# Layer 0's expert tiles in an order written out by hand, and one logarithm per image in the preparation for the scans

## The chip, the core and the metric

The kernel runs on one core of one Trainium2 chip, as one program. Its engines are called PE (matrix multiplication; its weight loads are shown apart, as PEld), DVE (vector), ACT (scalar functions), POOL (GpSimd) and SP (which issues DMAs). The metric is the device time of one execution in microseconds (us); lower is better.

## The reference

Four images of 256 channels and 32 × 32 pixels pass through two layers; each is a token mixer followed by a mixture of experts, and all is float32.

- Layer 0 mixes by attention with a kept set of scores, a depthwise convolution and a projection. Layer 1 mixes by four selective scans over the pixels (along rows and columns, forward and back), whose results are averaged.
- A mixture of experts normalizes each token, chooses two of eight experts for it, and adds their weighted results to the token: 256 to 256 to 256 features in layer 0, 256 to 1024 to 256 in layer 1.

The part that the change touches, in short:

```
# layer 0's experts
h = gelu(tokens @ w1[e] + b1[e])
y = h @ w2[e] + b2[e]
out = out + combine[:, e] * y

# the selective scan of layer 1
delta = softplus(x @ W_delta + b_delta)     # log(1 + exp(.))
Bm, Cm = x @ W_B, x @ W_C
dA  = exp(delta * -exp(A_log))
dBx = (delta * x) * Bm
h   = scan(dA, dBx)                         # h[l] = dA[l] * h[l-1] + dBx[l]
y   = sum_n(h * Cm) + x * D
```

## The kernel before

**Layout.** Channels lie on the 128 partitions in two halves (CT = 2), the 1024 pixels of an image along them, often in two halves of 512 (NHALF). An image is 8 blocks of 128 tokens (NT).

**Stages.** The attention of all images runs until about 1900 us of the span, layer 0's normalization, routing and scatter until about 2045, the 36 expert tiles of layer 0 until about 2276, the scans until about 3560, layer 1's experts and the end after that.

**Who sets the order.** A tile framework takes the program as written and, outside marked stretches, lets a planner order the instructions of all engines by priorities and a model of their costs. Inside `tc.manual_schedule()` each engine keeps the order of the source. Before the change, only the scans (L1792) are such a stretch. Each engine runs its own queue in order; semaphores join the queues. Tiles of a pool with `bufs=n` rotate through n buffers, and a new use waits for the last reader of the old one. Pools opened after others were closed take over their memory.

**Routing and scatter (L1244, L1123, L1498).** For each image, the tokens are normalized, their experts chosen, and POOL copies each token by indirect DMA to two slots in DRAM (`slots_x0`), grouped by expert.

**The tiles of layer 0 (`tile0`, L1507 to L1550).** A tile is 256 slots of one expert. SP reads the block's number and the expert's into registers and loads the tokens `xs` (L1514) and the two weights `w` (L1517, L1519). DVE copies the expert's biases (L1521, L1523) and works out the weight of each token (L1525 to L1528). PE transposes the tokens (`tp`, L1532), DVE copies them (`xe`, L1534); PE multiplies by w1 (`hp`, L1539), ACT takes the gelu (`hid`, L1540); PE multiplies by w2 (`yp`), DVE adds the bias (`ys`, L1546), ACT multiplies by the token's weight (L1548), DVE combines with the token where its best expert is this one (L1549), and SP stores the block to `slots_y0` (L1550). `xs` and `ys` have 4 buffers, the weights 3.

**The streams beside the tiles (L1565 to L1581).** Python generators whose steps are written between the tiles, four per tile. From tile 15 on there is `whole(0)`: the 16 gathers of image 0 from `slots_y0` on POOL (`fetched`, L1444, two per step; the first eight write, the others add), eight empty steps, and the transposes of the result with their addition to the image (`completed`, L1459; `op` at L1464). It is followed by the preparation of image 0 for its scans (`Prep.steps`, L1332). From tile 23 on there is `whole(1)`. Images 2 and 3 are gathered during the first scans.

**The preparation (`Prep.steps`, L1332 to L1442, 40 steps).** It normalizes the image over its channels: means on PE (L1341), squares on ACT, variances on PE, a power on POOL (L1359) refined on DVE, the scale spread by PE (`rb`), then the products with W_B and W_C (`bp`). The rest is softplus, worked out as relu(z) + log(1 + exp(-|z|)) with a correction for what rounding 1 + v loses: with v = exp(-|z|), `lost` forms v + 1 and the part of v that the sum dropped. For each channel half: PE forms z (`zp`), ACT takes Relu, Abs and Exp, DVE `lost` (L1419 to L1421), ACT one Ln over 128 × 1024 (L1430), DVE and POOL add up delta (L1434, L1435). Last, POOL forms dx = delta * x (L1393) and DVE adds x * D (L1394).

**The scans (L1739 to L1796).** Each of the 128 turns runs the scans of one image, channel half and state: column, forward and backward scans on DVE (L1697, L1671, L1680), exponentials on ACT, the products `uu` (L1658) and `da_c` (L1691) on POOL, sums on PE. The preparation of the next image runs beside them, two steps per turn, from an image's first turn for image 1 and from its ninth for images 2 and 3.

Of the kernel before, what the change touches and what calls it, by code (L numbers as in the profile page):

```python
# [11 lines left out]
F32 = mybir.dt.float32  # L12
# [9 lines left out]
P = 128  # L22
# [39 lines left out]
def metaformer(ctx: ExitStack, tc: tile.TileContext, t: dict, out: bass.AP):  # L62
# [1259 lines left out]
    class Prep:  # L1322
# [9 lines left out]
        def steps(self, room, psum, tag):  # L1332
# [44 lines left out]
            bc = room("sp", [4 * HALF])[: 2 * NS, :L]  # L1377
# [12 lines left out]
            def rest(c):  # L1390
                for h in range(NHALF):
                    cols = ts(h, HALF)
                    nc.gpsimd.tensor_tensor(self.dx[:, c, cols], self.delta[:, c, cols], xm[:, c, cols], ALU.mult)  # L1393
                    nc.vector.scalar_tensor_tensor(x[b][:, c, cols], xm[:, c, cols], dsk[:, c : c + 1],  # L1394
                                                   x[b][:, c, cols], ALU.mult, ALU.add)
                    yield
                    yield

            behind = iter(())
            for c in range(CT):  # L1400
                sp = room("sp", [4 * HALF]).rearrange("p (k n) -> p k n", k=4)

                def begin(h):
                    cols = ts(h, HALF)
                    zp = psum.tile([P, HALF], F32, tag=tag, name="zp")
                    for k in range(CT):
                        nc.tensor.matmul(zp, wd[:, k, ts(c, P)], xm[:, k, cols],
                                         start=(k == 0), stop=(k == CT - 1))
                    next(behind, None)
                    yield  # L1410
                    nc.scalar.activation(self.delta[:, c, cols], zp, AF.Relu, bias=bd[:, c : c + 1])
                    nc.scalar.activation(sp[:, h], zp, AF.Abs, bias=bd[:, c : c + 1])
                    nc.scalar.activation(sp[:, h], sp[:, h], AF.Exp, scale=-1.0)
                    next(behind, None)
                    yield

                def lost(h):
                    v, up, dd = sp[:, h], sp[:, 2 + h], self.dx[:, c, ts(h, HALF)]
                    nc.vector.tensor_scalar(up, v, 1.0, None, ALU.add)  # L1419
                    nc.vector.scalar_tensor_tensor(dd, up, 1.0, v, ALU.subtract, ALU.subtract, reverse1=True)  # L1420
                    nc.vector.scalar_tensor_tensor(v, v, 2.0, dd, ALU.subtract, ALU.mult)  # L1421

                yield from begin(0)
                yield from begin(1)
                for _ in behind:
                    pass
                lost(0)
                lost(1)
                yield
                nc.scalar.activation(sp[:, 2:], sp[:, 2:], AF.Ln)  # L1430
                yield
                for h in range(NHALF):
                    dd = self.delta[:, c, ts(h, HALF)]
                    nc.vector.scalar_tensor_tensor(dd, sp[:, h], -0.5, dd, ALU.mult, ALU.add)  # L1434
                    nc.gpsimd.tensor_tensor(dd, dd, sp[:, 2 + h], ALU.add)  # L1435
                yield
                yield
                behind = rest(c)
            for _ in behind:
                yield  # L1440
            yield
            yield  # L1442
# [31 lines left out]
    with ExitStack() as st:  # L1474
        wp = st.enter_context(tc.tile_pool(name="m0_w", bufs=1))
        pb = st.enter_context(tc.tile_pool(name="m0_b", bufs=2))
# [3 lines left out]

        b1 = load(wp, "b1_0", [P, E, CT])
        b2 = wp.tile([P, E, C], F32, tag="b2_0", name="b2_0")
        nc.sync.dma_start(b2, t["b2_0"].rearrange("e d -> (e d)").partition_broadcast(P).rearrange(
            "p (e d) -> p e d", e=E))
        tokens = [wp.tile([P, NT, W0], F32, tag=f"tok{b}", name=f"tok{b}") for b in range(B)]
        scattered = nc.alloc_semaphore("scattered")
        for b in range(B):
            d = pb.tile([P, CT, L], F32, tag="d", name="d")
            here = slot0[:, :, ts(b, NT)]
            for _ in norm(b, 0, tokens[b], pb, ps_n, "t", "t", d):  # L1490
                pass
            for _ in route(b, 0, tokens[b], here, wp.tile([P, 2560], F32, tag="numbers", name="numbers"), ps_n, "t"):
                pass

            with tc.tile_critical(name=f"scatter{b}", no_gpsimd_drain=True):
                for n in range(NT):
                    for k in range(2):
                        nc.gpsimd.indirect_dma_start(  # L1498
                            out=slots_x0, out_offset=bass.IndirectOffsetOnAxis(ap=here[:, k, n : n + 1], axis=0),
                            in_=tokens[b][:, n], in_offset=None).then_inc(scattered, 16)  # L1500
                nc.gpsimd.wait_ge(scattered, 16 * 2 * NT * (b + 1))
                if b == B - 1:
                    nc.clear_and_free_semaphores([scattered])

        blocks_x, blocks_y = (a.rearrange("(k a p) c -> k p a c", a=T // P, p=P) for a in (slots_x0, slots_y0))

        def tile0(i):  # L1507
            def register(k, most, engines):
                return nc.values_load(every.which[0:1, k, i : i + 1], engines=engines, min_val=0, max_val=most,
                                      skip_runtime_bounds_check_because="the minimum with that of a count")  # L1510

            block = register(1, E * BLOCKS, [mybir.EngineType.SP])
            xs = pb.tile([P, T // P, W0], F32, tag="xs", name="xs", bufs=4)
            nc.sync.dma_start(xs, blocks_x[bass.ds(block, 1)].rearrange("o p a c -> p (o a) c"))  # L1514
            e = register(0, E - 1, [mybir.EngineType.SP, mybir.EngineType.DVE])
            w1 = pb.tile([P, CT, C], F32, tag="w1", name="w1", bufs=3)
            nc.sync.dma_start(w1, t["w1_0"][bass.ds(e, 1)].rearrange("o (c p) f -> p (o c) f", p=P))  # L1517
            w2 = pb.tile([P, CT, C], F32, tag="w2", name="w2", bufs=3)
            nc.sync.dma_start(w2, t["w2_0"][bass.ds(e, 1)].rearrange("o (c p) f -> p (o c) f", p=P))  # L1519
            b1e = pb.tile([P, CT], F32, tag="b1e", name="b1e")  # L1520
            nc.vector.tensor_copy(b1e, b1[:, bass.ds(e, 1)].rearrange("p o c -> p (o c)"))  # L1521
            b2e = pb.tile([P, C], F32, tag="b2e", name="b2e")
            nc.vector.tensor_copy(b2e, b2[:, bass.ds(e, 1)].rearrange("p o d -> p (o d)"))  # L1523
            best = pb.tile([P, T // P], F32, tag="best", name="best")
            nc.vector.tensor_scalar(best, xs[:, :, C], every.expert[:, i : i + 1], None, ALU.is_equal)  # L1525
            wt = pb.tile([P, T // P], F32, tag="wt", name="wt")
            nc.vector.tensor_tensor(wt, best, xs[:, :, C + 1], ALU.mult)
            nc.vector.tensor_tensor(wt, wt, xs[:, :, C + 2], ALU.add)  # L1528
            tp = ps1.tile([P, CT, T], F32, tag="tp", name="tp")
            for a in range(T // P):  # L1530
                for c in range(CT):
                    nc.tensor.transpose(tp[:, c, ts(a, P)], xs[:, a, ts(c, P)], ident)  # L1532
            xe = pb.tile([P, CT, T], F32, tag="xe", name="xe")
            nc.vector.tensor_copy(xe, tp)  # L1534
            hp = ps_h.tile([P, CT, T], F32, tag="hp", name="hp")
            hid = pb.tile([P, CT, T], F32, tag="hid", name="hid")
            for f in range(CT):
                for c in range(CT):
                    nc.tensor.matmul(hp[:, f], w1[:, c, ts(f, P)], xe[:, c], start=(c == 0), stop=(c == CT - 1))  # L1539
                nc.scalar.activation(hid[:, f], hp[:, f], AF.Gelu, bias=b1e[:, f : f + 1])  # L1540
            yp = ps1.tile([P, T // P, C], F32, tag="yp", name="yp")
            for a in range(T // P):
                for f in range(CT):
                    nc.tensor.matmul(yp[:, a], hid[:, f, ts(a, P)], w2[:, f, :], start=(f == 0), stop=(f == CT - 1))
            ys = pb.tile([P, T // P, C], F32, tag="ys", name="ys", bufs=4)
            nc.vector.tensor_tensor(ys, yp, b2e.unsqueeze(1).to_broadcast([P, T // P, C]), ALU.add)  # L1546
            for a in range(T // P):
                nc.scalar.mul(ys[:, a], ys[:, a], wt[:, a : a + 1])  # L1548
                nc.vector.scalar_tensor_tensor(ys[:, a], xs[:, a, :C], best[:, a : a + 1], ys[:, a], ALU.mult, ALU.add)  # L1549
# [463 lines left out]
```

## Time and profile before

| | |
|---|---|
| Median of 3 runs | 4160.04 us (4149.68 to 4175.9) |
| Profiled execution | 4157.79 us, span 4155.8 us, 50303 instructions |
| PE busy | 3518.4 us (85%) |
| DVE busy | 3041.4 us (73%) |
| ACT busy | 2847.3 us (69%) |
| POOL busy | 1823.3 us (44%) |
| Tiles of layer 0 | about 2045 to 2276 us of the span |
| Scans | about 2276 to 3560 us of the span |

How to read it: times in the views are us, and the share of busy time is of the whole span, so it averages stages with different limits. "idle before <-releaser" is the time in which an engine stood still ahead of an instruction, and what ended it. SPq, POOLq and the like are the queues of an engine that issue DMAs. A stretch is a part of the span between two times in us; its columns are the length, the busy time of each engine with the number of instructions, the clock granted to PE as a share of full speed, the busy share of the DMA engines, and GB/s. Lines of the time line give start, length, engine, source line, operation and operands, the number of equal neighbours, and in brackets the idle time before them. Lines of the waits give the waiting instruction, what it waited for, the total, the number of times and the longest.

### The profile page before, as it was taken

The page shows a single profiled execution, that of the slowest core. Times are in us where ns is not written, and L with a number is a line of the kernel's source. Part 1 is how long each engine was busy: PE and PEld are TensorE (multiplying, and loading weights), DVE is VectorE, ACT ScalarE, POOL GpSimd, SP SyncE. Part 2 cuts the span into 40 slices and gives each one's busy share as a digit, 9 for nine tenths or more (in the row PEclk, how much of TensorE's full clock was granted, in tenths as well). Part 3 has the DMA queues.
Part 4 walks back from the last instruction along what each step waited for, and adds up shares of the span by engine and source line. Part 5 has one row for each costly group of instructions (what it writes and reads, how often), then busy time and mean ns, then how long its engine had stood idle before and what let it go on. Part 6 is the DMA issues. An engine that isn't in the chain of part 4 may idle for free. (4 is left out here: it accounts for less than half of the span.)

```text
span 4155.8 us, 50303 instructions
## 1 busy us (share of the span) xinstructions
PE 3518.4 (85%) x17502; PEld 1949.6 (47%) x17502; DVE 3041.4 (73%) x5327; ACT 2847.3 (69%) x3823; POOL 1823.3 (44%) x1436
## 2 busy tenths in 40 slices
PE   8378878888888888866487999999999999999996
PEld 5144434444444444433365434443443434688885
DVE  2689899989898989883356889899899899411112
ACT  2889999999999999963235667767667677422222
POOL 0146454554455445562323666446446546221111
PEclk9568888788778877977698999999999999999997
DMA  9300093009000000001375334333333334565565
GB/s 289 92 1 1 1 263 79 1 1 306 32 1 1 11 1 1 11 1 45 118 200 167 120 104 132 102 107 114 109 100 114 118 103 136 185 186 184 188 196 184
DMA packets 280986, 426.37 MB, mean 103 GB/s; under 512 B 31889, under 2 KB 223634, under 8 KB 280594
## 3 DMA queue, kind: packets, MB, share of 16 engines
q1 hardware_dynamic: 259920, 382.66, 30.3%
q0 software_dynamic: 17024, 38.98, 3.0%
q8 instruction: 141, 2.31, 0.2%
q10 hardware_dynamic: 3778, 1.41, 0.1%
q14 instruction: 123, 1.01, 0.1%
HBM read 280.34 MB, written 142.64 MB: 102 GB/s over the span
## 5 line engine op out<-in xcount | busy, mean ns | idle before, releaser
L490 POOL TENSOR_SCALAR dr<-s_n,last 128x1024 bf16<-128x1024 f32 x256 | 732.1, 2878 | 853.9 <-DVE state L518 435.4
L406 ACT ACTIVATE junk_a<-s_n,state 128x1024 int8<-128x1024 f32 x448 | 514.6, 1149 | 25.4 <-DVE state L518 6.8
L1691 POOL TENSOR_TENSOR da_c<-prod,come 128x1024 f32<-128x1024 f32 x128 | 248.1, 1938 | 386.7 <-DVE h L1697 381.9
L410 DVE TENSOR_SCALAR_CACHE_REDUCE junk_v<-s_n,state 128x1024 int8<-128x1024 f32 x320 | 408.7, 1277 | 8.8
L1861 ACT ACTIVATE hid<-hp,b 128x256 f32<-128x256 f32 x288 | 133.7, 474 | 355.1 <-PE hp L1859 354.6
L457 DVE SCALAR_TENSOR_TENSOR w<-s_n,win 128x1024 f32<-128x1024 f32 x256 | 351.4, 1373 | 5.3
L460 DVE MAX8 win<-w 128x8 f32<-128x1024 f32 x256 | 314.5, 1228 | 8.8
L1658 POOL TENSOR_TENSOR uu<-dx,bb 128x1024 f32<-128x1024 f32 x128 | 304.9, 2382 | 1.0 <-DMA bb<-bc_d 1.0
L558 ACT ACTIVATE ex<-sT 128x1024 f32<-128x1024 f32 x256 | 247.0, 1015 | 84.5 <-PE sT L550 84.4
L1697 DVE TENSOR_TENSOR_SCAN h<-da_c,uu 128x1024 f32<-128x1024 f32 x128 | 302.8, 2366 | 0.0
L406 ACT ACTIVATE junk_a<-s_n,guess 128x1024 int8<-128x1024 f32 x256 | 294.2, 1149 | 7.4
L1671 DVE TENSOR_TENSOR_SCAN h<-da,uu 128x1024 f32<-128x1024 f32 x128 | 290.8, 2272 | 4.2 <-POOL uu L1658 4.2
L1680 DVE TENSOR_TENSOR_SCAN h<-da,uu 128x1024 f32<-128x1024 f32 x128 | 289.8, 2264 | 0.0
L568 PE MATMUL o_ps<-ex,vT 128*32 128x256 f32 x2048 | 238.1, 445 | 45.4 <-ACT ex L558 37.4
L1701 PE MATMUL hp<-h,ident 128*128 128x512 f32 x512 | 248.9, 609 | 31.1 <-DVE h L1697 30.6
L1645 ACT ACTIVATE da_c<-delta,a_log 128x1024 f32<-128x1024 f32 x128 | 268.2, 2096 | 0.2
L1859 PE MATMUL hp<-xe,w 128*128 128x256 f32 x1152 | 258.6, 381 | 6.1 <-DVE xe L1847 5.9
L1666 PE MATMUL hp<-da_c,ident 128*128 128x512 f32 x512 | 247.0, 605 | 18.2 <-POOL da_c L1691 16.3
L440 ACT COPY s_n<-sp 128x1024 f32<-128x1024 f32 x256 | 245.6, 1004 | 24.4 <-PE sp L432 12.5
L1870 DVE TENSOR_TENSOR ys<-yp,b2e 128x512 f32<-128x512 f32 x36 | 24.9, 691 | 321.1 <-PE yp L1867 321.1
L1666 PE MATMUL hp<-h,twice 128*128 128x512 f32 x512 | 243.8, 599 | 17.3 <-issue 13.4
L1659 ACT COPY uu<-uu 128x1024 f32<-128x1024 f32 x128 | 254.5, 1988 | 3.4 <-POOL uu L1658 3.4
(542 smaller groups left out, 7519.8 us busy)
## 6 DMA issues: line engine op xcount, KB each, us to landing
bb<-bc_d SPq DMA_DIRECT2D x128, 512.0 KB
cb<-bc_d SPq DMA_DIRECT2D x128, 512.0 KB
w<-in_w SPq DMA_DIRECT2D x36, 1024.0 KB
w2e<-in_w SPq DMA_DIRECT2D x36, 1024.0 KB
slots_x<-zeros SPq DMA_DIRECT2D x1, 33411.0 KB
slots_x<-zeros SPq DMA_DIRECT2D x1, 33282.0 KB
slots_y<-zeros SPq DMA_DIRECT2D x1, 33024.0 KB
w<-in_w SPq DMA_DIRECT2D x72, 256.0 KB
```

Source lines behind the costliest of these rows:

```text
L406: nc.scalar.activation(junk, self.row(r), AF.Sign, bias=thr, scale=-1.0, accum_out=u)
L410: nc.vector.tensor_scalar(junk, self.row(r), thr, None, ALU.is_lt, ALU.add, accum_out=u)
L457: nc.vector.scalar_tensor_tensor(w, self.row(r), self.win[:, r, 0:1], self.row(r), ALU.is_gt if r < LAST_DVE else ALU.is_ge, ALU.subtract, ...
L460: nc.vector.max(out=self.win[:, r, 1:], in_=w)
L490: ins = nc.gpsimd.tensor_scalar(dr, self.row(r), self.last[:, r : r + 1], None, ALU.is_lt)
L1645: nc.scalar.activation(grid(self.da_c), cols_flipped(self.prep.delta[:, self.c]), AF.Exp, scale=self.decay)
L1658: nc.gpsimd.tensor_tensor(self.uu[:, 0], self.prep.dx[:, self.c], self.bb, ALU.mult)
L1666: nc.tensor.matmul(self.hp[h], ident if eye is None else eye, view[:, ts(h, HW // NHALF), :], start=first, stop=last)
L1671: nc.vector.tensor_tensor_scan(rows.rearrange("p r w -> p (r w)"), self.da, self.uu[:, 0], 0.0, ALU.mult, ALU.add)
L1680: nc.vector.tensor_tensor_scan(hs[:, ::-1], self.da[:, ::-1], self.uu[:, 0][:, ::-1], 0.0, ALU.mult, ALU.add)
L1697: nc.vector.tensor_tensor_scan(hs, self.da_c, self.uu[:, 1], 0.0, ALU.mult, ALU.add)
L1859: nc.tensor.matmul(hp[:, f % 2], self.w1[:, c, ts(f, P)], self.xe[:, c], start=(c == 0), stop=(c == CT - 1))
```

## The change

It has two parts.

1. **The tiles.** `tile0` becomes a class `Tile0` with six steps (`load`, `turned`, `small`, `hidden`, `result`, `store`), and the 36 tiles and their streams stand in `tc.manual_schedule()`. Iteration i writes hidden(i), store(i-1), turned(i+1), result(i), small(i+1), load(i+3), and then three steps of each stream that has begun. `store` issues its DMA from POOL, which loads the block's number itself; DVE loads the expert's number with an instruction of its own. `xs` has 6 buffers, the weights 4, `ys` 8. `whole` gathers four per step. The normalization, routing and scatter use pools of their own, closed before those of the tiles are opened, with a smaller `numbers`.
2. **The preparation.** The four parts (channel half, pixel half) run in one sequence: `lost` takes two DVE instructions and leaves the lost part in dx; one Ln covers 128 × 2048 and adds the one itself (`bias=1.0`); the additions, the product dx and the addition to x are on DVE alone. It has 44 steps.

```diff
-            behind = iter(())
-            for c in range(CT):
-                sp = room("sp", [4 * HALF]).rearrange("p (k n) -> p k n", k=4)
...
-                def lost(h):
-                    v, up, dd = sp[:, h], sp[:, 2 + h], self.dx[:, c, ts(h, HALF)]
-                    nc.vector.tensor_scalar(up, v, 1.0, None, ALU.add)
-                    nc.vector.scalar_tensor_tensor(dd, up, 1.0, v, ALU.subtract, ALU.subtract, reverse1=True)
-                    nc.vector.scalar_tensor_tensor(v, v, 2.0, dd, ALU.subtract, ALU.mult)
...
-                nc.scalar.activation(sp[:, 2:], sp[:, 2:], AF.Ln)
-                yield
-                for h in range(NHALF):
-                    dd = self.delta[:, c, ts(h, HALF)]
-                    nc.vector.scalar_tensor_tensor(dd, sp[:, h], -0.5, dd, ALU.mult, ALU.add)
-                    nc.gpsimd.tensor_tensor(dd, dd, sp[:, 2 + h], ALU.add)
+            parts = [(c, ts(h, HALF)) for c in range(CT) for h in range(NHALF)]
+            v = room("sp", [CT, L])
+
+            def lost(c, cols):
+                back = self.dx[:, c, cols]
+                nc.vector.tensor_scalar(back, v[:, c, cols], 1.0, 1.0, ALU.add, ALU.subtract)
+                nc.vector.tensor_tensor(back, v[:, c, cols], back, ALU.subtract)
+
+            for i, (c, cols) in enumerate(parts):
+                zp = psum.tile([P, HALF], F32, tag=tag, name="zp")
+                for k in range(CT):
+                    nc.tensor.matmul(zp, wd[:, k, ts(c, P)], xm[:, k, cols], start=(k == 0), stop=(k == CT - 1))
+                if i:
+                    lost(*parts[i - 1])
                 yield
+                nc.scalar.activation(self.delta[:, c, cols], zp, AF.Relu, bias=bd[:, c : c + 1])
+                nc.scalar.activation(v[:, c, cols], zp, AF.Abs, bias=bd[:, c : c + 1])
+                nc.scalar.activation(v[:, c, cols], v[:, c, cols], AF.Exp, scale=-1.0)
                 yield
+            lost(*parts[-1])
+            yield
+            nc.scalar.activation(v, v, AF.Ln, bias=1.0)
+            yield
+            for c, cols in parts:
+                dx = self.dx[:, c, cols]
+                nc.vector.tensor_tensor(dx, dx, v[:, c, cols], ALU.add)
+                nc.vector.tensor_tensor(self.delta[:, c, cols], self.delta[:, c, cols], dx, ALU.add)
                 yield
                 yield
+                nc.vector.tensor_tensor(dx, self.delta[:, c, cols], xm[:, c, cols], ALU.mult)
+                nc.vector.scalar_tensor_tensor(x[b][:, c, cols], xm[:, c, cols], dsk[:, c : c + 1],
+                                               x[b][:, c, cols], ALU.mult, ALU.add)
                 yield
...
+        class Tile0:
...
+            def load(self):
+                block = self.register(1, E * BLOCKS, [mybir.EngineType.SP])
+                self.xs = pb.tile([P, T // P, W0], F32, tag="xs", name="xs", bufs=6)
...
+            def store(self):
+                for a in range(T // P):
+                    nc.scalar.mul(self.ys[:, a], self.ys[:, a], self.wt[:, a : a + 1])
+                    nc.vector.scalar_tensor_tensor(self.ys[:, a], self.xs[:, a, :C], self.best[:, a : a + 1],
+                                                   self.ys[:, a], ALU.mult, ALU.add)
+                block = self.register(1, E * BLOCKS, [mybir.EngineType.Pool])
+                nc.gpsimd.dma_start(blocks_y[bass.ds(block, 1)].rearrange("o p a c -> p (o a) c"), self.ys)
...
-            yield from fetched(b, y, range(NHALF), 2)
+            yield from fetched(b, y, range(NHALF), 4)
...
+        with tc.manual_schedule():
+            tiles = [Tile0(i) for i in range(USUAL)]
+            for i in range(AHEAD):
+                tiles[i].load()
+            tiles[0].turned()
+            tiles[0].small()
+            for i in range(USUAL):
+                tiles[i].hidden()
+                if i > 0:
+                    tiles[i - 1].store()
+                if i + 1 < USUAL:
+                    tiles[i + 1].turned()
+                tiles[i].result()
+                if i + 1 < USUAL:
+                    tiles[i + 1].small()
+                if i + AHEAD < USUAL:
+                    tiles[i + AHEAD].load()
+                for first_tile, steps in beside:
+                    if i >= first_tile:
+                        for _ in range(3):
+                            next(steps, None)
```

## The prediction

> **What bounds the kernel now.** I read the page's 40 slices first (each 103.9 us), to see which engine leads where the change lies: the tiles of layer 0 (2045 to 2276 us) are slices 20 and 21, the scans (2276 to 3560) the twelve that follow. The fences below are, in order: the page, busy time by stretch, the time line, the waits between 2050 and 2275, and three more cuts of the time line.
>
> ```profile
> span 4155.8 us, 50303 instructions
> ...
> PE   8378878888888888866487999999999999999996
> ...
> DVE  2689899989898989883356889899899899411112
> ...
> POOL 0146454554455445562323666446446546221111
> ```
>
> In slices 20 and 21 PE reads 8 and 7, in the scans 9 throughout, with DVE at 8 and 9. So the scans have little left to give, and the tiles have some. The stretches (busy us of PE, PEld, DVE, ACT, POOL) show where:
>
> ```profile
> 2060.00:2120.00 60.00, 56.28 (x268) 45.59 (x268) 39.86 (x122) 22.89 (x53) 0.00 (x0) 1.00 0.78 231
> 2120.00:2160.00 40.00, 26.01 (x117) 19.88 (x116) 17.18 (x48) 9.61 (x22) 20.21 (x16) 0.87 0.69 181
> 2200.00:2240.00 40.00, 28.19 (x121) 20.36 (x121) 28.41 (x59) 29.49 (x41) 20.85 (x15) 0.91 0.59 144
> 2800.00:2900.00 100.00, 91.77 (x208) 38.22 (x207) 96.99 (x78) 74.63 (x56) 66.91 (x47) 1.00 0.35 117
> ```
>
> Alone, the tiles keep PE at 94%; once the streams beside them start (2120), at 65 to 70%. In steady state a tile takes 4.35 us: from one hp matmul to the next (2104.14 and 2108.49 in the time line) while its own PE work is 0.43 (tp) + 1.73 (hp) + 1.73 (yp) = 3.9. The source order of the change chains five steps, which this cut prices:
>
> ```profile
> 2104.14 1.13 PE L1539 MATMUL hp<-xe,w 128*128 128x256 f32 x4 [0.19 <-ACT hid L1540]
> 2105.31 0.47 ACT L1540 ACTIVATE hid<-hp,b1e 128x256 f32<-128x256 f32 x1 [0.43 <-PE hp L1539]
> 2108.34 0.89 ACT L1548 ACTIVATE ys<-ys,wt 128x256 f32<-128x256 f32 x2
> 2109.01 0.87 DVE L1549 SCALAR_TENSOR_TENSOR ys<-xs,best,ys 128x256 f32<-128x256 f32 x2
> 2108.41 0.68 DVE L1534 COPY xe<-tp 128x512 f32<-128x512 f32 x1
> ```
>
> What stops PE beside the streams is the gathered rows that it transposes. The second line is the other way about: POOL stood idle before the power that the normalization needs, so nothing was queued ahead of it.
>
> ```profile
> PE op L1464 <- DMA y<-slots_y,slot: 15.8, 9, 7.9
> POOL ln_r L1359 <- DVE ln_ve L1356: 15.3, 1, 15.3
> ```
>
> ```profile
> 2127.47 0.99 POOL L1451 DMA_INDIRECT y<-slots_y,slot  x1 [84.17 <-DVE ys L1549]
> 2136.48 0.95 POOL L1451 DMA_INDIRECT y<-slots_y,slot  x1 [0.30 <-issue]
> 2142.38 1.60 POOL L1451 DMA_INDIRECT y<-slots_y,slot  x1 [4.96 <-DVE b2e L1523]
> 2159.36 0.40 SPq L1550 DMA_DIRECT2D slots_y<-ys  x1
> ```
>
> Stores and gathers order each other: the first gather waits for a store, and a store held at 2139.44 (the issue before this last one) came 2.0 us after the last gather began, the next gather 2.94 after that store. One gather costs 0.97 + 0.30 = 1.27 us, one that adds 1.54 + 0.30 = 1.84.
>
> **Part 1, the tiles.** Order per iteration: hp(i), store(i-1), tp(i+1), yp(i), small(i+1), loads of i+3. On ACT the gelu of i stands before the two multiplications of i-1; on DVE the last step of i-1 before the copy xe(i+1), which hp(i+1) needs. The loop is hp 1.73 + 0.20 to start the gelu + 0.37 for it + 0.94 for the multiplications + 0.40 for the second combination + 0.73 for the copy = 4.37 us, against 4.35 before: nothing won. From ys(0) at 2058, ys(35) comes 35 × 4.37 = 153 later, at 2211, if nothing stood beside. What stands beside adds:
>
> - Image 0's gathers, twelve in one iteration, four in the next: store(14) on POOL 2.9 us to land, 8 × 1.27, 4 × 1.84, store(15) waiting for the gathers before it, then four more. PE's order is fixed, so the transposes of y hold every tile behind them: 5.7 + 8.2 by my replay, with their own work **+15** (before: 7.9 in the longest wait).
> - The means and variances, 16 matmuls like the 3.60 us row for the eight of ln_mean, in tiles 21 to 24: **+9.3**.
> - The power (L1359, 1.69 us) is issued behind image 1's first twelve gathers (8 × 1.27 + 4 × 1.84 = 17.5 us) and a store; DVE's next step waits for it and with it every copy xe: **+16**. Before, the planner had it at 2172.20, ahead of that image's gathers at 2187.
> - rb and bp **+4.2**; ACT, which the loop now runs through, carries Relu, Abs, Exp and about 7 table loads of 1.28 us (before 14) in tiles 28 to 31: **+12.6**; image 1's additions **+2**; the last DVE parts **+2**; the rest of the streams **+2.6**.
>
> Sum 63.7: the last ys at 2274.7. To this come 2.15 (its multiplications and combinations, as before from 2271.82 to 2273.97), 0.6 for the store on POOL, 2.9 to land and 1.7 for the set-up of the scans: they begin at 2282, before at 2276.3. **+6**, give or take 12.
>
> Not shown by the trace is a plain store issued by POOL. Above it stands a gather (0.99, an adding one 1.69), below SP's store (0.40); I take 0.6, nearest to a plain write that POOL issues at the end of the kernel (0.54). A gain from SP's freed queue is excluded in steady state: its loads already run three tiles ahead. At 1.69, 36 of them are 61 us of POOL, of which only the four among gathers and the last lie open: +5.5. The DVE register load costs 0.31 against the same load before, so nothing. Deeper buffers (xs 6, w 4, ys 8) cost nothing.
>
> At this place the Trainium skill speaks against the change: "DMA: Bandwidth & Descriptors", section "SWDGE vs HWDGE vs iDMA", puts plain transfers on SP or ACT, and the page's table has about 1 us to the first byte from GpSimd against 0.6. By it the five exposed stores would be an estimated 2 us later, all 36 an estimated 14. The 2.94 us row is of a store on SP; no row here has one on POOL.
>
> **Part 2, the preparation** (four images, three of them beside scans). Removed per image: four POOL additions of 2.41 mean and four products of 1.28 (14.8 us, about 12 of them on top of POOL's work in the scans), two Ln of 1.06 and one pair of table loads (2.6). Added: one Ln of twice the size (about the same 2.1 together) and on DVE, per part, two additions and one product of 0.60 pitch for what were a combination; `lost` loses one of three steps. Net DVE, 4 × (3 - 1 - 1) × 0.60 = **+2.4**. Against it stands contention, which this cut shows:
>
> ```profile
> 2813.82 2.28 DVE L1697 TENSOR_TENSOR_SCAN h<-da_c,uu 128x1024 f32<-128x1024 f32 x1
> 2822.88 3.36 DVE L1697 TENSOR_TENSOR_SCAN h<-da_c,uu 128x1024 f32<-128x1024 f32 x1
> 2822.52 4.79 POOL L1435 TENSOR_TENSOR delta<-delta,sp 128x512 f32<-128x512 f32 x2 [0.40 <-DVE delta L1434]
> ```
>
> The same scan takes 2.28 alone and 3.36 beside POOL's addition; all such rows of one image add up to 8.1 us. So DVE gains 8.1 - 2.4 = 5.7, ACT 2.6. PE is the cover's end: 91.77 busy of 100 in the stretch from 2800, so about 8.2 can be won there at most. Two prep steps go into each turn, 44 for 40, so the window grows by two turns at no cost of its own. I take 6 for each of three images: **-18**. Bounds: -6 (table loads alone, 2 each) and -30 (8.2 each, and the 15.10 us turn of image 0 cut to a neighbour's 9).
>
> The skill's "GPSIMD Engine Reference", section "Key points", says that POOL shares its SBUF interfaces with VectorE, so that instructions with two SBUF inputs contend. The rows agree for the scan. By that rule the twelve new two-input instructions on DVE would suffer beside POOL's other work too, by the scan's ratio (3.36 to 2.28) an estimated 0.3 us each. No row here has one of that size surely beside POOL, and I count none.
>
> **Sum.** The profiled execution took 4157.8 (span 4155.8); 4157.8 + 6 - 18 = **4146**. The median of the runs, 4160.0, lies 2.2 above it, and I leave that out.
>
> **Rivals.** *Faster: the gathers don't bite.* Before, PE waited 15.8 us in nine waits; if the replay holds the fixed order too hard (y[0] there when PE comes, the power ahead of image 1's gathers), +15 and +16 go: the stage ends 25 us early, the scans give 20, together about 4111. For it speaks that eight buffers of ys for four and a fourth of w let tiles run ahead of a late store; against it, that PE meets the transposes in a fixed place.
>
> *Slower: the loop of a tile grows.* After ys(i) DVE loads a register and copies b1e, and gelu(i+1) needs it: 0.69 + 0.31 + 0.17 = 1.2 after yp's end, while the second half of hp lets the first gelu start as late as 1.4 after it. Above this the loop itself lengthens: each 0.33 us more is 12 us over 36 tiles. At +0.4 us it takes back the whole forecast gain; at 5.0 us a tile, +22, the time is 4168; at 5.9, +55, it is 4201. For it: the 0.28 us idle before that copy even now; against it: 0.2 us of room.
>
> *It does not do what it says:* the planner's order was all but the source's (period 4.35 against 4.37), and the streams cost what they cost. Then only the scans count: 4140.
>
> **How the numbers follow.** Forecast 0.59 (4118 to 4180), faster rival 0.18, slower rival 0.14, no change of order 0.09. One per cent is 41.6 us, about what a measurement of this kernel can tell from no change; measured from the median, faster begins at 4118.4 and slower at 4201.6. Faster: 0.18 and 0.02 from the forecast's edge, 0.20. Slower: the upper half of its rival and 0.02 from streams that are worse, 0.09. Same 0.71. The range reaches to the faster rival's 4108 and half into the slower one, 4190.
>
> **What would show it.** The tiles: L1546's counterpart 4.3 to 4.4 us apart until tile 15, a wait of 5 to 8 us of PE on each y, and DVE waiting some 16 us for the power. Scans beginning at 2270 to 2294. In the scans no POOL work from the preparation, the column scan at 2.3 throughout, the windows of images 1 and 2 some 6 us shorter. Wrong it would be if a tile takes 5 us or more alone, or if the gathers start so early that PE meets them done.

## The result

The changed kernel takes 4194.16 us (median of 11 runs, 4182.15 to 4206.79), the kernel before 4160.04 in the same comparison (4147.12 to 4175.9): ratio 1.0083, 95% interval 1.0063 to 1.0102. It is 34 us slower where 14 us faster was forecast, and the time lies outside the range of 4108 to 4190.

The page of the changed kernel, the same rows as before:

```profile
span 4191.9 us, 50266 instructions
...
PE   8378878788888888865477799999999999999996
...
DVE  2689898989898989873344789899899999411112
...
POOL 0146454554455445562332565445445546221111
```

Each slice is now 104.8 us. The tiles of layer 0 fill more than two slices: behind the 8 of the seventeenth, PE reads 6, 5, 4, 7, 7, 7 where it read 6, 6, 4, 8, 7, 9. Where the time lies is told by four marks of the time line: the first and the last `ys` of the tiles, the first column scan and the last.

| us of the span | before | after | difference |
|---|---|---|---|
| up to the first ys | 2057.65 | 2065.47 | +7.8 |
| first ys to last ys (36 tiles) | 214.2 | 251.0 | +36.9 |
| last ys to first column scan | 16.0 | 24.3 | +8.3 |
| first to last column scan | 1268.8 | 1252.2 | -16.5 |
| the rest | 599.2 | 598.8 | -0.4 |

The first row is not the change: from the first scatter of image 0 to the first ys it is 121.6 us before and 120.3 after, so the 9 us arise in the attention, whose code is the same. In the kernels below, all with the same attention, the first ys comes anywhere from 2048 to 2073. Stages are therefore compared, not spans. Without the first row the two profiles differ by 28 us, which fits the interval of the ratio (26 to 42 us).

The tiles, in the same columns as the stretches of before:

```profile
2065.00:2125.00 60.00, 49.87 (x227) 36.27 (x225) 32.20 (x104) 19.14 (x44) 7.94 (x11) 1.00 0.63 195
...
2145.00:2185.00 40.00, 27.47 (x116) 19.71 (x116) 18.40 (x55) 8.70 (x20) 22.63 (x19) 0.90 0.69 180
```

With nothing beside them and the clock at 1.00, the tiles keep PE busy 83% of the time; it was 94%. A tile takes 5.35 us, tile after tile, where 4.37 was reckoned. The time line of PE and of ACT over one tile says why:

```profile
2097.24 1.13 PE L1538 MATMUL hp<-xe,w 128*128 128x256 f32 x4 [0.31 <-DVE xe L1518]
2098.98 1.13 PE L1538 MATMUL hp<-xe,w 128*128 128x256 f32 x4 [0.61 <-ACT hid L1540]
2099.95 0.60 PE L1516 MATMUL tp<-ident,xs 128*128 128x128 f32 x4
2100.39 1.89 PE L1546 MATMUL yp<-w,hid 128*128 128x256 f32 x8
```

```profile
2098.46 0.47 ACT L1540 ACTIVATE hid<-hp,b1e 128x256 f32<-128x256 f32 x1 [2.39 <-DVE wt L1530]
2100.15 0.47 ACT L1540 ACTIVATE hid<-hp,b1e 128x256 f32<-128x256 f32 x1 [1.22 <-PE hp L1538]
2100.52 0.89 ACT L1553 ACTIVATE ys<-ys,wt 128x256 f32<-128x256 f32 x2
```

The two halves of `hp` lie in one PSUM tile. The matrix products of the second half do not start (2098.98) until the gelu has read the first half (2098.46 + 0.47). So hp isn't one block of 1.73 us with a tail: from its start to the start of the second gelu are 1.22 + 0.52 + 1.17 = 2.91 us, in place of 1.93. This is in the loop of every tile: 2.91, then 0.37 to the multiplications, 0.53 to the combination (2101.05), 0.80 to the copy xe (2101.85), 0.74 to the next hp (2102.59), together 5.35.

The wait was there before, and in sight: in the prediction's own fence, the row of hp at 2104.14 carries "[0.19 <-ACT hid L1540]". There the planner had put the four transposes of the next tile between the two halves (2107.70, ahead of the same row one tile later, at 2108.49), so that 0.19 was left of the wait.

### The profile page after: what moved, and what is told of

Its sections match the earlier page's. It is cut to its first block, busy times and chain, and to the rows that moved or that the text cites. A ratio compares the mean times of both kernels' runs of the same rounds, so it can differ in the third digit from the quotient of the medians.

```text
span 4191.9 us, 50266 instructions
## 1 busy us (share of the span) xinstructions
PE 3541.8 (84%) x17502; PEld 1959.3 (47%) x17502; DVE 3022.6 (72%) x5343; ACT 2827.7 (67%) x3806; POOL 1787.8 (43%) x1440
## 5 line engine op out<-in xcount | busy, mean ns | idle before, releaser
L1723 DVE TENSOR_TENSOR_SCAN h<-da_c,uu 128x1024 f32<-128x1024 f32 x128 | 291.0, 2274 | 0.0
L1893 PE MATMUL yp<-w2e,hid 128*128 128x256 f32 x1152 | 255.9, 379 | 0.0
```

The costliest lines, as they stand in the source:

```text
L1723: nc.vector.tensor_tensor_scan(hs, self.da_c, self.uu[:, 1], 0.0, ALU.mult, ALU.add)
L1893: nc.tensor.matmul(yp[:, a], self.hid[:, f, ts(a, P)], self.w2[:, f, :], start=(f == 0), stop=(f == NF - 1))
```

## The experiments

**Which wait makes the tile 5.35 us.** Theory A: the one PSUM tile of both halves, in a loop that runs through ACT and DVE. Theory B: the gelu is late because DVE's small steps are; the waits name a `wt` step of DVE (L1530) ahead of 17 gelus, 43.6 us in all. Three edits, the third both of the others.

```diff
 # two PSUM tiles
-                hp = ps_h.tile([P, CT, T], F32, tag="hp", name="hp")
                 for f in range(CT):
+                    hp = ps_h.tile([P, HALF], F32, tag="hp", name="hp", bufs=3)[:, :T]
 # copy first
-                if i > 0:
-                    tiles[i - 1].store()
                 if i + 1 < USUAL:
                     tiles[i + 1].turned()
+                if i > 0:
+                    tiles[i - 1].store()
                 tiles[i].result()
```

> The changed kernel, with the two halves of hp in two PSUM tiles (three buffers of one bank) instead of one tile. Theory A (one tile: the second half of hp waits until the gelu has read the first, and the loop of a tile runs through that wait: 1.22 + 0.53 + 1.17 us instead of 1.73 + 0.20): the wait of 0.61 us ahead of the second half goes, a tile takes 4.37 us instead of 5.35, the time falls by 35 x 0.98 = 34 us, to about 4160. Theory B (the gelu is late because DVE's small steps of the tile are late, as the waits of ACT on L1531 say): a tile still takes 5.3 us, 4194.

> The changed kernel, with turned(i+1) written ahead of store(i-1), so that DVE copies xe(i+1) before it waits for ACT's multiplications; hp stays one tile. Theory A: the loop through ACT and DVE is cut, and the tile takes what PE needs with the wait between the halves of hp: 1.75 + 0.87 + 0.43 + 1.73 = 4.8 us, 0.57 less, 35 times: 20 us, to about 4174. Theory B: unchanged, 4194.

> Both edits: two PSUM tiles for hp, and turned(i+1) ahead of store(i-1). Theory A: neither the loop nor the wait is left, PE alone sets the tile at 3.9 to 4.0 us: 35 x 1.4 = 49 us less than the changed kernel, about 4145. Theory B: unchanged, 4194.

| | us of one tile, expected by A | measured | first to last ys | ratio to before (95%) |
|---|---|---|---|---|
| changed kernel | | 5.35 | 251.0 | 1.0083 (1.0063 to 1.0102) |
| two PSUM tiles | 4.37 | 4.47 | 230.6 | 1.0016 (0.9992 to 1.0040) |
| copy first | 4.8 | 4.78 | 242.5 | 1.0070 (1.0044 to 1.0096) |
| both | 3.9 to 4.0 | 3.89 | 227.1 | 1.0006 (0.9985 to 1.0026) |

Theory A stands for the undisturbed tile: each edit takes from it what it was priced at. The stage and the whole time gain less (forecast were 4160, 4174 and 4145 us, ratios of 1.000, 1.003 and 0.996). Two PSUM tiles take 0.88 us from a tile, 31 us over 35 tiles, but 20.4 from the stage: what stands beside the tiles then adds 74 us to the loop, for 64 in the changed kernel.

With two PSUM tiles hp is one row of eight again, and the gelu still has the same DVE step named as its releaser, with the same 2.39:

```profile
2101.51 1.99 PE L1538 MATMUL hp<-xe,w 128*128 128x256 f32 x8 [0.31 <-DVE xe L1518]
2102.73 0.48 ACT L1540 ACTIVATE hid<-hp,b1e 128x256 f32<-128x256 f32 x1 [2.39 <-DVE wt L1530]
```

In the kernel with the copy first, the gelu of a tile starts ahead of the `wt` step of the same tile:

```profile
2103.05 0.47 ACT L1540 ACTIVATE hid<-hp,b1e 128x256 f32<-128x256 f32 x1 [1.81 <-PE hp L1538]
2103.27 0.16 DVE L1530 TENSOR_TENSOR wt<-best,xs 128x2 f32<-128x2 f32 x1
```

Theory B has fallen: the gelu does not need this step, as it starts 0.22 us ahead of it here. (That it starts 1.22 after hp both in the changed kernel and with two PSUM tiles proves nothing by itself, as the `wt` step stands 0.98 after hp in both.) The 0.1 us by which 4.47 exceeds 4.37 is in the start of the second gelu, 2.03 from the start of hp in place of 1.93: the eight rows of hp take 1.99 us behind PE's wait of 0.31, and 1.89 in the kernel with both edits, where PE does not wait.

With both edits PE does nothing but work in the undisturbed tiles, but the stage is only 3.5 us shorter than with two PSUM tiles alone. Of the 0.58 us a tile that copying first adds, the first sixteen tiles should give 9. The rest went into a wait that grew, as the waits of PE in the kernel with both edits show:

```profile
PE op L1445 <- DMA y<-slots_y,slot: 23.9, 8, 14.2
...
PE ln_rb L1371 <- DVE ln_rs L1364: 19.0, 1, 19.0
```

The first of these was 5.5 us in the changed kernel and 8.5 with two PSUM tiles alone; the second was 6.5 and 15.7. The faster the tiles, the earlier PE's fixed order meets the transposes of gathered rows, and the gathers are no sooner done.

A wait of PE costs more than its own length here. Behind the waits for y in this kernel the eight rows of hp take 3.00 and 3.62 us (at 2167.50 and 2179.86, at a granted clock of 0.60 and 0.50) for 1.89 otherwise. Over the part of the stage with streams, the clock granted to PE averages 0.93 before (from 2120), 0.87 in the changed kernel (from 2145) and 0.84 with both edits (from 2131). The prediction had no term for this, and no run separates it from the waits.

**What the streams cost.** Theory C: these waits are a matter of where the steps are written. Rival D: the work beside the tiles has its length, whatever the order. Both runs start from the kernel with both edits.

```diff
 # streams re-timed
-            yield from pause(8)
+            yield from pause(24)
-        beside = [(FIRST, chain(whole(0), preps[0].steps(room, ps_n, "t"))), (SECOND, whole(1))]
+        beside = [(FIRST, chain(whole(0), preps[0].steps(room, ps_n, "t"))), (SECOND + 4, whole(1))]
-                        for _ in range(3):
+                        for _ in range(4):
 # power first: of these lines only
+        beside = [(FIRST, chain(whole(0), preps[0].steps(room, ps_n, "t"))), (SECOND + 3, whole(1))]
```

> Both edits of the run before (two PSUM tiles for hp, turned(i+1) ahead of store(i-1)), and the streams re-timed: four steps per tile instead of three (so that all 16 gathers of an image are issued in one iteration), 24 empty steps behind the gathers instead of 8, image 1's stream from tile 27 instead of 23. Theory C (PE's fixed order meets the transposes of y before the gathers are done, and the power stands behind image 1's gathers on POOL): the waits of PE for y, 24 us in the run with both edits, and DVE's wait for the power, about 10, go; with closer steps some of it is lost again: about 4145. Rival D (what stands beside the tiles has its own length, whatever the order): the stage stays at 227 us, 4175.

> Both edits, and only image 1's stream moved, from tile 23 to tile 26, so that the power of image 0's normalization is issued on POOL ahead of image 1's gathers. Theory C: the tile of 24 us among the last third falls by 11 to 16, about 4162. Rival D: the gathers hold PE later instead, 4175.

Re-timed: ratio 0.9971 (0.9947 to 0.9995), first to last ys 215.6 us. Power first: 0.9976 (0.9951 to 1.0002), 213.1 us, 14 less than with both edits. In the re-timed kernel 0.3 us is left of PE's wait for y (23.9 us with both edits) and half of that for the power (9.4 us, from 20.5); but the stage is only 11.5 us shorter. The rest went into the denser steps: besides the tile with the wait for the power (18.7 us), three of the last third take 12.5 to 16.3 us. With image 1's stream moved back alone, DVE waits 1.9 us for the power (20.5 with both edits), and PE still waits 18.5 us for y. Theory C holds: the waits go where the steps are moved. D has a part in it: beyond them, the steps themselves stretch the tiles.

**The end of the stage.** The scans' constants stood behind the hand-ordered stretch. This shows in the time line of the changed kernel, where the load of A_log, issued at 2324.96, its exponential and its sign precede the first exponential of the scans:

```profile
2329.41 0.23 ACT L1631 ACTIVATE a_log<-a_log 128x32 f32<-128x32 f32 x1 [2.79 <-DMA a_log<-in_a_log]
2329.67 1.97 DVE L1632 TENSOR_SCALAR a_log<-a_log 128x32 f32<-128x32 f32 x1 [0.91 <-ACT a_log L1631]
...
2331.68 2.03 ACT L1671 ACTIVATE da_c<-delta,a_log 128x1024 f32<-128x1024 f32 x1 [2.04 <-DVE a_log L1632]
```

In the experiment they are made ahead of the tiles, in a pool that is open there (`sw`):

```diff
     nc.gpsimd.memset(power, -0.5)
+    am = load(sw, "a_log", [P, CT, NS])
+    nc.scalar.activation(am, am, AF.Exp)
+    nc.vector.tensor_scalar(am, am, -1.0, None, ALU.mult)
+    twice = sw.tile([P, P], F32, tag="twice", name="twice")
...
```

> The changed kernel, with the scans' constants (the load of A_log, its exponential and sign, twice the identity, the reset mask) made ahead of the tiles instead of behind them. If the scans begin late because these constants queue behind the hand-ordered stretch, the time from the last ys to the first column scan falls from 24.3 to about 17 us, the whole to about 4187. Rival (the landing of the last store, issued by POOL, sets the begin): 4194, unchanged.

Measured: 1.0053 (1.0031 to 1.0074), and from the last ys to the first column scan 19.6 us instead of 24.3. Of the 8.3 us that the change adds here, 4.7 are the constants. For the rest the time line has this: between the last ys (2316.51) and its combination (2319.83) DVE does the last steps of the preparation, and the last store is issued at 2321.76, 5.25 us after the last ys, where before it was 2.2 (2274.00 after 2271.82).

**The queue of the stores.** POOL's two lines in `store` were given back to SP:

```diff
-                block = self.register(1, E * BLOCKS, [mybir.EngineType.Pool])
-                nc.gpsimd.dma_start(blocks_y[bass.ds(block, 1)].rearrange("o p a c -> p (o a) c"), self.ys)
+                block = self.register(1, E * BLOCKS, [mybir.EngineType.SP])
+                nc.sync.dma_start(blocks_y[bass.ds(block, 1)].rearrange("o p a c -> p (o a) c"), self.ys)
```

> The changed kernel, with the stores of the tiles issued by SP again instead of POOL. If the issuing queue is what costs (0.4 us more for each store, all 36 exposed): 14 us less, 4180. If only the stores among the gathers and the last lie open: 2 us less, 4192. If a store on SP that waits for gathers holds the loads behind it for longer than three tiles: up to 10 us more, 4204.

Measured: 1.0085 (1.0058 to 1.0112), the same as the changed kernel. The tiles take 7 us more (258.0), the end 1.8 less (22.5), and in this profile the scans no less. A store's issue is 0.40 us on SP and 0.71 on POOL. What SP loses is seen in its queue and on PE. A store that waited for the gathers is issued at 2159.14, the loads behind it follow, and PE waits for the tokens:

```profile
2159.14 0.40 SPq L1557 DMA_DIRECT2D slots_y<-ys  x1
2160.05 0.37 SPq L1505 DMA_DIRECT2D xs<-slots_x  x1
```

```profile
2162.88 1.08 PE L1516 MATMUL tp<-ident,xs 128*128 128x128 f32 x4 [8.90 <-DMA xs<-slots_x]
...
2175.34 1.08 PE L1516 MATMUL tp<-ident,xs 128*128 128x128 f32 x4 [6.15 <-DMA xs<-slots_x]
```

A tile with nothing beside it still takes 5.35 us, so the issue of 36 stores was not what cost. The expectation of held loads has its part, and so has the last store, and in the whole time they cancel. The rule of the Trainium skill that plain transfers belong on SP or ACT ("DMA: Bandwidth & Descriptors", "SWDGE vs HWDGE vs iDMA") is neither confirmed nor refuted in time: the two queues come out even here.

**The preparation alone**, in the kernel before:

> The kernel before with the change's preparation alone, the tiles as before. If the two parts are independent, the scans give 16 to 17 us as between the two profiles, and the tiles a few us for the fewer table loads: about 4142. Rival (the scans were shorter because the new order leaves images 0 and 1 in another state at their begin): no gain, 4160.

Measured: 0.9957 (0.9937 to 0.9977), 17 to 18 us; first to last column scan 1251.9 us, first to last ys 213.9. The few us that fewer table loads should have given the tiles are not there (214.2 before). The two parts of the change are independent: this part wins what it wins in the changed kernel, and the other loses the rest.

**Versions that beat both.** All edits of the order together, with an image's gathers issued in one iteration (`fetched(..., 6)`); and, the other way, the kernel before with the new preparation and two PSUM tiles for hp, its order left to the planner.

> The changed kernel with two PSUM tiles for hp, turned(i+1) ahead of store(i-1), image 1's stream from tile 26, all 16 gathers of an image issued in one iteration, and the scans' constants made ahead of the tiles. By the single runs: 4153 of the run with image 1's stream moved, less 5 for the constants, less up to 8 for gathers that no store stands between: about 4141, faster than the kernel before (4160) and than the preparation alone (4150). If what stands beside the tiles only moves, 4150.

> The kernel before with the change's preparation and two PSUM tiles for hp, the order of the tiles left to the planner. If the wait between the halves also costs there what the source order showed, the tile falls from 4.35 towards 3.9 us: 17 undisturbed tiles x 0.45 = 8 us less than with the preparation alone, about 4142. If the planner had filled that wait already with the transposes and yp of another tile: 4150, the same.

The first measured 0.9936 (0.9916 to 0.9957), the second 0.9928 (0.9911 to 0.9944): both faster than the kernel before by 0.6 to 0.7% (by the medians 23 and 29 us, where 19 and 18 were forecast), and not told apart. By hand a tile takes 3.89 us and the stage 203.6, with one tile of 26 us left where PE waits for y; the planner's tile falls from 4.35 to 4.08, its stage stays at 213.2 (213.9 with the preparation alone), and its end is 2.4 us shorter than by hand (16.6 for 19.0). So two PSUM tiles shorten the planner's undisturbed tile too, but waits beside the later tiles take that back: PE waits 18.9 us for y, for 15.8 in the kernel before. Whether they help the whole time is open, since the intervals of the preparation alone and of this version overlap.

## Why the prediction was wrong

**The step that failed is the first term of part 1**, "hp 1.73 + 0.20 to start the gelu". It took hp for one block of work and put 1.93 us from its start to the second gelu; 2.91 were measured, because the second half waits for the gelu of the first. With two PSUM tiles, 2.03 are left. The loop was then 5.35 us, not 4.37; over 35 tiles that is the 34.3 us by which the stage missed the forecast (251.0 for 216.7). The sum of the other terms held: first ys to last was put at 216.7 us, 153 of it loop, and 251.0 - 35 × 5.355 = 63.6 stands against 63.7.

**The terms inside that sum** did less well. By the excess of each group of tiles over 5.355: image 0's gathers 14.4 (put at 15), means and variances 14.1 (9.3), the power 9.3, with a wait of 11.0 (16), rb and bp 3.4 (4.2), the tiles with ACT's softplus work and image 1's additions 22.6 (14.6), the last four 0.3 (4.6). That they cancel is luck. PE waited 5.5 us in all for y, where the replay had 5.7 + 8.2; the rest of the 14.4 is in other waits of the same tiles and in PE's lower clock behind them (four rows of hp take up to 2.07 us for 1.13). The wait for the power is where it was said to be, on POOL behind image 1's gathers:

```profile
DVE ln_rr L1361 <- POOL ln_r L1359: 11.0, 1, 11.0
...
PE op L1445 <- DMA y<-slots_y,slot: 5.5, 4, 2.3
```

**The end of the stage** was put at 2.8 us more than before (7.3 from the last ys to the scans' first cumulative sum, for 4.5); it is 5.5 more there (10.0), and 8.3 at the first column scan. The 1.7 for the set-up left out that the load of A_log, its exponential and its sign now stand in line (4.7 us at the first column scan) and put 2.15 for the last tile's multiplications and combinations, which took 4.2 (2316.51 to 2320.70) with steps of the preparation among them. Put at 0.6, the issue of a store on POOL measured 0.71.

**The scans** were right: -18 forecast, -16.5 between the profiles and some 17 in the run with this part alone. The turns of images 0, 1 and 2 are 4.0, 6.4 and 5.5 us shorter, where 6 each was forecast. The column scans that took 3.36 to 3.64 us before are all at 2.26 to 2.29:

```profile
2860.22 2.29 DVE L1723 TENSOR_TENSOR_SCAN h<-da_c,uu 128x1024 f32<-128x1024 f32 x1
2870.52 2.28 DVE L1723 TENSOR_TENSOR_SCAN h<-da_c,uu 128x1024 f32<-128x1024 f32 x1
```

The sum of all 128 fell by 11.8 us: 4.8 each in the turns of images 1 and 2, which carry the preparations of images 2 and 3, and 2.2 in those of image 0. The rest of the 8.1 per image that the prediction gave to contention is in the short scans between them (`come`, 128 × 32), which took 1.58 and 1.94 us beside POOL's product dx and 0.21 otherwise:

```profile
2884.14 1.94 DVE L1686 TENSOR_TENSOR_SCAN come<-prod,gap 128x32 f32<-128x32 f32 x1
```

They fell by 3.2 us in the turns of image 1 and by 3.3 in those of image 2, so the 8.1 is borne out for two of the three windows; in the first it was 3.2. The cover named for it was right too: in the same eight turns (the 49th to the 56th), before and after, PE is busy 81.07 of 86.2 us and then 80.31 of 80.4:

```profile
2779.00:2865.20 86.20, 81.07 (x186) 34.13 (x185) 79.49 (x68) 65.11 (x53) 51.60 (x37) 1.00 0.31 112
```

```profile
2828.00:2908.40 80.40, 80.31 (x186) 34.34 (x185) 72.89 (x64) 62.46 (x50) 43.93 (x32) 1.00 0.38 120
```

**The rivals.** The slower one said that the loop of a tile would grow, priced it (5.0 us a tile: 4168, 5.9: 4201), and comes nearest: 5.35 lies between. Its mechanism was another, the copy of b1e, and that isn't what grew: with the halves apart the copy stands where it stood, and the tile is 0.88 us shorter. The faster rival held that the gathers bite less than the replay says. In the changed kernel they do: PE waits 5.5 us for y, and 15.8 in the kernel before. But its tiles are slow; with faster ones the wait is back (23.9 with both edits).

Two small readings in the prediction are off, without weight for its sum: the store held at 2139.44 came 2.0 us after the end of the last gather's issue, not after its beginning, and 4157.8 - 25 - 20 is 4113, not 4111.

## What to carry to other kernels

When an order is written out by hand, a wait that the planner had filled can come back at full size (here 0.19 us became 0.61, and 0.98 in the loop): look in the old trace for waits of an instruction on the reader of its own tile, however short, and price the loop with them open. Two halves that are written and read in turn by two engines are worth trying in two PSUM tiles. A fixed order has to be re-timed whenever its parts become faster, since what it meets (gathers, a power on another engine) keeps its own pace.

## What was not expected

Whether a scan lost time beside POOL went with where its operands lie; no run moved an operand to test it. In the kernel before, the scan at 2822.88 reads `da_c` and `uu`, both in SBUF, and took 3.36 us beside POOL's addition; the next one reads `da`, which lies in PSUM, and ran beside POOL's work (the product `uu` at 2829.35 and others) without loss:

```profile
2826.17 2.26 DVE L1671 TENSOR_TENSOR_SCAN h<-da,uu 128x1024 f32<-128x1024 f32 x1
2828.35 2.26 DVE L1680 TENSOR_TENSOR_SCAN h<-da,uu 128x1024 f32<-128x1024 f32 x1
```

In the changed kernel, some scans with an operand in PSUM run wholly beside POOL's tensor instructions (the one at 2422.85 beside three of them) and still take 2.27. This agrees with the Trainium skill's "GPSIMD Engine Reference", section "Key points", which speaks of DVE instructions with two SBUF inputs. The new additions and products on DVE took 0.66 to 0.74 us in the scans; they lay beside the issues of gathers and scatters on POOL at most, never beside a tensor instruction, so that no row tells what they would have lost.

Whether the wait between the halves of hp belongs to the PSUM tile or to the bank in which both lie is open: in the runs, each of the two tiles had a bank of its own. Four tiles of half a bank each, which would tell, did not fit beside the other pools of PSUM (8 KB per partition where three banks were left), so there is no time for them.
